# A recurrent layer and a gated wavelet layer: the first two steps' input product taken raw in fp32 column tiles

## The chip, the core and the metric

The kernel runs on one core of a Trainium2 chip. A core has five engines with instruction queues of their own: TensorE (PE in the profile, with its weight loads as PEld), VectorE (DVE), ScalarE (ACT), GpSimd (POOL) and SyncE (SP), which here only issues transfers. They meet at semaphores. Matmuls write into PSUM, eight banks of 128 partitions by 512 fp32 values; everything else lies in SBUF, 128 partitions wide, or in device memory, reached by 16 DMA engines.

The metric is the time of one execution on the device, in microseconds. Smaller is better.

## What is computed

There are 64 sequences of 256 steps with 1024 features each. The first layer is a recurrence with a residual, the second a Haar decomposition whose parts are all scaled by one gate and put together again, with a residual too:

```python
# layer 0
xW = jnp.einsum('ntd,dh->nth', x, Wx) + b
xW_t = jnp.swapaxes(xW, 0, 1)
def step(prev_h, xw):
    next_h = jnp.tanh(prev_h @ Wh + xw)
    return (next_h, next_h)
_, h_t = jax.lax.scan(step, h0, xW_t)        # h0 = cond_1024
x = x + jnp.swapaxes(h_t, 0, 1)
# layer 1
h = jax.nn.silu(q_pool @ W1.T + b1)          # q_pool = cond_1024
gate = jax.nn.sigmoid(h @ W2.T + b2)[:, None, :]
...
a = a * gate
for dc in reversed(details):
    dc = dc * gate
    e = (a + dc) * INV_SQRT2
    o = (a - dc) * INV_SQRT2
...
return v + a
```

Since every part of the decomposition is scaled by the same gate, layer 1 is a multiplication of x by 1 + gate. The kernel computes it so (its `factor` is that gate plus 1, times the residual of layer 0). What remains in order is the recurrence: step t needs the h of step t-1.

## The kernel before

**Layout.** Features lie on the partitions. A "pair" is two steps of all 64 sequences: a tile of 128 partitions by 1024, `pairs[i]`. T is 256 steps, NP 128 pairs, B = 8 blocks of 128 features, G = 2 groups of 32 sequences, Q = 4 quarters of 256 output features.

**Two ways to multiply.** A *column-tile* product (`plain_product`) takes 32 columns of its input as the stationary operand, and puts quarter q of the output on partitions 32q to 32q+31, so four quarters can stand in the array beside each other. One call covers one block k of features with 8 matmuls of 256 columns in fp32; the profile records each fp32 matmul twice. A *split* product (class `XWork`) cuts x and Wx into a high part and a scaled low part, types them for the faster fp32r matmul, and adds three products: main = x0·wx0 + x1·wx1, mixed = x2·wx2. One block is six matmuls of 128x512 and covers both steps of the pair; a pair is 48 of them. `split_weight` makes the three forms of a block of Wx, overwriting the raw block: on DVE L116, L133 and L135, on ACT L132 and L134. The constructor of `XWork` does the same for x (L116, L273, L275, and L281 on ACT in `begin`).

**From the split product to a step.** `take_mixed` scales the mixed banks into `sum` on ACT (L289) and POOL adds the bias row b_row (L290); `finish` adds the main banks on DVE (L321), writes `sum` to device memory and reads it back by eight transfers in the layout of h (L325, L331). `put` copies the result of one step into the bank `acc` (L225).

**A step.** `h_product` multiplies h by Wh with seven Strassen products of 32 records each into the banks acc, m16 and m57 (L183): products 1, 2, 5, 6, 7, 4, 3 in this order. Product 1 goes to m16, is copied by ACT into y[0] (L236), and product 6 is then accumulated in m16. DVE adds the parts (L242, L245, L249); ACT takes tanh (L426); DVE transposes (L428) and forms the four sums for the next step (`strassen_sides`, L213 to L216); POOL adds h to x (L455). The weights' own sums are made once: t5 from `first` (L164), t6, b12 and t4 from `others` (L164, L175, L164).

**The order.** PE's order is that of the program text throughout, DVE's until `in_order` is closed after step 0; a scheduler orders the rest. Between two step products PE works on the next pair: `first` (24 split matmuls) after an odd step, `second` (24) after an even one, so that a step's chain on DVE and ACT has something beside it. Step 0 has no Strassen product: `h_block` multiplies h0 by Wh in column tiles between the split blocks of pair 0. `gate_block` loads one block of W1 and multiplies h0 by it into `gate_ps`; `gate_hidden` applies b1 and silu, one block of W2 follows in each of steps 1 to 8, and `gate_factor` ends the gate.

**Buffers and queues.** A pool hands a tag's buffers out again when their last reader is done: tag `t` has six (raw Wx 0 to 5, then t5, t6, t4), `slab` six (x pairs, raw Wx 6 and 7, W1 and W2 blocks), `y` one (b1's tile first, then each step's y), `xw` three. Nearly all transfers are issued by SP in one order, with at most eight under way, since each takes the semaphore of the eighth before it; h0T, b_row and the tiles of b1 and b2 (eight small transfers each) are issued by ACT.

Of the kernel before, what the change touches and what calls it, by code (L numbers as in the profile page):

```python
# [59 lines left out]
P = 128  # L60
# [19 lines left out]
def tile_cond_resid(  # L80
# [26 lines left out]
    def slab(name: str):  # L107
        return slabs.tile([P, D], F32, tag="slab", name=name)

    def load_x(i: int) -> None:  # L110
        pairs[i] = slab(f"x{i}")
        nc.sync.dma_start(out=pairs[i], in_=xT[i])
# [9 lines left out]
    def load_weight(k: int):  # L122

        raw = sums_tile(f"wx{k}") if k < 3 * KB // 2 else slab(f"wx{k}")
        nc.sync.dma_start(out=raw, in_=wx[k])
        return raw

    def split_weight(raw, k: int) -> list:

        w0 = high_bits(raw[:], f"wx_high{k}")  # L130
        three = [wpool.tile([P, D], F32R, tag=f"wx{i}", name=f"wx{i}_{k}") for i in range(3)]
        nc.scalar.copy(three[0], w0)  # L132
        nc.vector.tensor_sub(raw, raw, w0)  # L133
        nc.scalar.activation(three[1], raw, AF.Copy, scale=UP)  # L134
        nc.vector.scalar_tensor_tensor(out=three[2], in0=raw, scalar=-UP, in1=w0, op0=ALU.mult, op1=ALU.add)  # L135
        return three

    def load_bias(v: bass.AP, pool, tag: str, name: str):
        t = pool.tile([P, G, F], F32, tag=tag, bufs=1, name=name)
        for q in range(Q):  # L140
            for g in range(G):
                nc.scalar.dma_start(out=t[q * R : (q + 1) * R, g, :], in_=v[q : q + 1, :].broadcast_to((R, F)))
        return t[:].rearrange("p g f -> p (g f)")

    def halves(w):
# [44 lines left out]
                    tile_position=(0, q * R),  # L190
                )

    def plain_product(ps, vT, w, k: int) -> None:

        for g in range(G):
            col = (g * B + k) * R
            for q in range(Q):


                nc.tensor.matmul(  # L200
                    out=ps[q * R : (q + 1) * R, g * F : (g + 1) * F],
                    lhsT=vT[:, col : col + R],
                    rhs=w[:, q * F : (q + 1) * F],
                    start=k == 0 and g == 0,
                    stop=k == B - 1,
                    skip_group_check=True,
                    tile_position=(0, q * R),
                )
# [10 lines left out]
    def flat(v):  # L219
        return v[:].rearrange("p i e -> p (i e)")  # L220
# [7 lines left out]
    def h_product(acc, a: dict, t: int):  # L228

        m16, m57 = (bank(f"m{i}", f"m{i}_{t}") for i in (16, 57))  # L230
        m16, m5, m7 = m16[:, :E], m57[:, :E], m57[:, E : 2 * E]
        part = [acc[:, i * E : (i + 1) * E] for i in range(3)]
        y = sums.tile([P, 4, E], F32, tag="y", bufs=1, name=f"y{t}")
        u = sums.tile([P, E], F32, tag="u", name=f"u{t}")
        strassen_product(m16, a[1], 1, True)
        nc.scalar.copy(y[:, 0], m16)  # L236
        strassen_product(part[0], a[2], 2)
        strassen_product(m5, a[5], 5, True)
        strassen_product(m16, a[6], 6)
        nc.scalar.copy(u, m16)  # L240
        strassen_product(m7, a[7], 7)
        nc.vector.tensor_add(  # L242
            y[:, 1:3], m57[:, : 2 * E].rearrange("p (i e) -> p i e", i=2), u[:].unsqueeze(1).broadcast_to((P, 2, E))
        )
        nc.vector.tensor_add(y[:, 3], m7, y[:, 1])  # L245
        strassen_product(part[2], a[4], 4)
        strassen_product(part[1], a[3], 3)
        h = work.tile([P, W], F32, tag="h", bufs=1, name=f"h{t}")
        nc.vector.tensor_add(h, acc, flat(y))  # L249
        return h  # L250

    def bank(tag: str, name: str):
        return one_pool.tile([P, HALF], F32, tag=tag, name=name)
# [81 lines left out]
            return xw  # L335


    h0T = const.tile([P, W], F32, tag="h0T", name="h0T")
    nc.scalar.dma_start(out=h0T, in_=condT)
    wh_raw = []  # L340
    b_row = const.tile([P, D], F32, tag="b_row", name="b_row")
    load_x(0)
    wx_raw, wx_s = [load_weight(k) for k in range(B)], []
    for k in range(B):
        wh_raw.append(wpool.tile([P, D], F32, tag="wh", name=f"wh_{k}"))
        nc.sync.dma_start(out=wh_raw[k], in_=wh[k])
    load_x(1)
    load_x(2)
    nc.scalar.dma_start(out=b_row, in_=b.broadcast_to((P, D)))
    b1_n = load_bias(b1, sums, "y", "b1_n")  # L350

    ctx.enter_context(tc.manual_schedule(engines={mybir.EngineType.PE}))
    in_order = ExitStack()
    in_order.enter_context(tc.manual_schedule(engines={mybir.EngineType.DVE}))
    now = XWork(0)
    now.begin()
    gate_ps = bank("gate", "gate_ps1")
    acc = bank("acc", "acc0")


    def h_block(k: int) -> None:
        plain_product(acc, h0T, wh_raw[k], k)

    def gate_block(k: int) -> None:
        w1 = slab(f"w1_{k}")
        nc.sync.dma_start(out=w1, in_=w1T[k])
        plain_product(gate_ps, h0T, w1, k)

    for k in range(B):
        wx_s.append(split_weight(wx_raw[k], k))  # L370
        now.block(k)
        if 3 <= k < 7:
            h_block(2 * k - 6)
            h_block(2 * k - 5)
    now.take_mixed()
    wh_s = StrassenWeight(wh_raw)
    wh_s.first()
    xw_next = now.finish()
    later = XWork(1)
    for k in range(B):  # L380
        gate_block(k)

    def gate_hidden(z):
        nc.vector.tensor_add(z, gate_ps, z)
# [26 lines left out]
        nc.gpsimd.tensor_mul(of_step(x, s), of_step(x, s), blocks(factor))  # L411

    h = work.tile([P, W], F32, tag="h", bufs=1, name="h0")
    nc.vector.tensor_add(h, acc, flat(xw_next[0]))
    now = later
    now.first()


    kept, again, factor = [], [], None
    for t in range(T):  # L420
        i, s = divmod(t, S)
        if s == 0:
            xw = xw_next
        if t:
            h = h_product(acc, sides, t)
        nc.scalar.activation(h, h, AF.Tanh)  # L426
        hT = work.tile([P, W], F32, tag="hT", name=f"hT{t}")
        nc.vector.transpose(hT, h)  # L428
        if t + 1 < T:
            sides = strassen_sides(hT, t)  # L430
        if t == 0:
            wh_s.others()
            g1T = gate_hidden(b1_n)
        if s == 0:
            acc = put(xw[1], t + 1)


        if s == 0 and i + 1 < NP:
            now.second()
            if i + 2 < NP:  # L440
                later = XWork(i + 2)
            xw_next = now.finish()
        if s == 1 and i + 2 < NP:
            now = later
            now.first()
        if s == 1 and i + 1 < NP:
            acc = put(xw_next[0], t + 1)

        if t == 0:
            in_order.close()  # L450


        x = pairs[i]
        if t + S < T:
            nc.gpsimd.tensor_add(of_step(x, s), of_step(x, s), blocks(hT))  # L455
        if 1 <= t <= B:
            k = t - 1
            if k == 0:
                gate_ps = bank("gate", "gate_ps2")
            w2 = slab(f"w2_{k}")  # L460
            nc.sync.dma_start(out=w2, in_=w2T[k])
            plain_product(gate_ps, g1T, w2, k)
            if k == B - 1:
                factor = gate_factor(load_bias(b2, const, "h0T", "b2_n"))
        if t + S >= T:

            for half in range(2):
                part = slice(half * KB, (half + 1) * KB)
                v = of_step(x, s)[:, :, part]
                nc.vector.tensor_add(v, v, blocks(hT)[:, :, part])  # L470
                nc.vector.tensor_mul(v, v, blocks(factor)[:, :, part])
                to = yT[i].rearrange("p (b s n) -> p s b n", b=B, s=S)[:, s, part]
                (nc.sync, nc.scalar)[half].dma_start(
                    out=to, in_=x[:].rearrange("p (b s n) -> p s b n", b=B, s=S)[:, s, part]
                )
        elif factor is not None:
            scale(x, s)
            if s == S - 1:
                nc.sync.dma_start(out=yT[i], in_=x)
        elif s == S - 1:  # L480
            kept.append(dram.tile([P, D], F32, tag="kept", bufs=B // S, name=f"kept{i}"))
            nc.sync.dma_start(out=kept[i], in_=x)
        if s == S - 1:
            del pairs[i]
            if i + 3 < NP:
                load_x(i + 3)


        if factor is not None and kept and i >= B and i % 4 < 2:
            if i % 4 == 0 and s == 0:  # L490
                again = slab(f"again{i}")
                nc.sync.dma_start(out=again, in_=kept[0])
            elif i % 4 == 1:
                scale(again, s)
                if s == 1:
                    nc.sync.dma_start(out=yT[i // 4 - B // 4], in_=again)
                    kept.pop(0)
# [28 lines left out]
```

## Time and profile before

| what | value |
| --- | --- |
| median of 3 runs | 3132.99 us (3133.29, 3128.22, 3132.99) |
| profiled execution | 3130.2 us, of which the span of its instructions is 3128.4 us |
| PE busy | 3080.6 us, 63648 matmul records |
| DVE, ACT, POOL busy | 1764.4, 718.7, 1113.9 us |
| DMA, mean over the span | 96 GB/s, 299.59 MB |
| first split matmul of pair 0 | 14.26 us |
| addition that starts h0 (DVE L414) | 52.08 us |
| first matmul of step 1's product | 70.14 us |
| first matmul of step 2's product, in the chain | 83.13 us |

A row of a timeline gives start, length, engine, line, operation, tiles written and read, and in brackets the engine's idle time before it with what ended it. A row of the chain that ended last gives start, length, and the engine or transfer on which the end rested. A row of a table of windows gives the window, its length, the busy time of the engine, the granted TensorE clock (1.00 is full speed), the share of the DMA engines and GB/s. PE's busy time overlaps itself, since matmuls are pipelined: for PE's pace the chain's lengths are used, not the single durations.

### The profile page before, as it was taken

Reading aid. Unit: us, or ns where it says so; the run is one execution under the profiler, and the core shown is the slowest. Engines: PE = TensorE matmul, PEld = TensorE weight load, DVE = VectorE, ACT = ScalarE, POOL = GpSimd, SP = SyncE. Lnnn points to the kernel's source line nnn. Section 1 sums busy time; section 2 is a strip of 40 time slices with the busy share of each in tenths; the row PEclk is TensorE's granted clock in tenths of the full one; section 3 lists DMA queues with packets and bytes.
Section 4 is the critical chain, followed back from the end, with each engine's and each line's share of the span. In section 5 each row is a group of like instructions: output and inputs, shape, how many; then the busy total and the mean of one; then the engine's idle time right before and its main releaser. Section 6 shows DMA issues by size and latency. Waiting matters only on the chain.

```text
span 3128.4 us, 137344 instructions
## 1 busy us (share of the span) xinstructions
PE 3080.6 (98%) x63648; PEld 2691.4 (86%) x63648; DVE 1764.4 (56%) x2736; ACT 718.7 (23%) x1425; POOL 1113.9 (36%) x768
## 2 busy tenths in 40 slices
PE   6999999999999999999999999999999999999998
PEld 4888888888888888888888888888888888888887
DVE  7455565555555555555555555555555555555554
ACT  3222222222222222222222222222222222222221
POOL 1233443333333333333333333333333333333332
PEclk9999999999999999999999999999999999999999
DMA  6332323222222222222222222222222222222222
GB/s 242 121 110 90 108 99 101 92 90 90 91 89 97 84 94 92 90 90 90 92 88 91 96 90 89 91 90 90 91 89 97 86 90 94 90 90 90 90 77 70
DMA packets 146573, 299.59 MB, mean 96 GB/s; under 512 B 25552, under 2 KB 91600, under 8 KB 146000
## 3 DMA queue, kind: packets, MB, share of 16 engines
q1 hardware_dynamic: 143888, 289.24, 27.3%
q8 instruction: 498, 8.16, 1.1%
q10 hardware_dynamic: 2112, 1.57, 0.2%
q14 instruction: 75, 0.61, 0.1%
HBM read 154.40 MB, written 136.31 MB: 93 GB/s over the span
## 4 chain that ended last, share of the span: by engine, by line
PE 95%; DMA 2%; DVE 1%; issue 1%; ACT 0%; SPq 0%; POOL 0%; ACTq 0%; DVEq 0%
PE main L257 29%; PE m L183 29%; PE acc L183 21%; PE mixed L257 15%; DMA sum_d<-sum 1%; DMA xw<-sum_d 1%; PE gate_ps L200 0%; DMA wx<-wx 0%; DMA w<-w1T 0%; PE acc L200 0%; DMA b_row<-b 0%; SPq L331 0%; DVE h L249 0%; DVE s L213 0%; ACT h L426 0%
## 5 line engine op out<-in xcount | busy, mean ns | idle before, releaser
L455 POOL TENSOR_TENSOR x<-x,hT 128x512 f32<-128x512 f32 x254 | 448.3, 1765 | 1691.2 <-DVE hT L428 1668.9
L257 PE MATMUL main<-wx,x 128*128 128x512 f32 x4096 | 990.5, 393 | 15.6 <-ACT wx L132 15.6
L257 PEld LDWEIGHTS main<-wx,x 128*128 128x128 f32 x4096 | 759.1, 188 | 196.5 <-issue 25.4
L242 DVE TENSOR_TENSOR y<-m,u 128x256 f32<-128x256 f32 x255 | 108.2, 425 | 872.4 <-PE m L183 872.4
L257 PE MATMUL mixed<-wx,x 128*128 128x512 f32 x2048 | 503.9, 398 | 2.1 <-DVE wx L135 2.1
L183 PE MATMUL m<-t,s 128*32 128x128 f32 x16320 | 493.4, 273 | 2.7 <-DVE s L215 2.7
L257 PEld LDWEIGHTS mixed<-wx,x 128*128 128x128 f32 x2048 | 374.4, 188 | 103.0 <-issue 25.8
L183 PEld LDWEIGHTS m<-t,s 128*32 128x32 f32 x16320 | 451.2, 110 | 3.5 <-issue 3.4
L290 POOL TENSOR_TENSOR sum<-sum,b_row 128x512 f32<-128x512 f32 x256 | 330.8, 1293 | 261.8 <-ACT sum L289 261.8
L426 ACT ACTIVATE h<-h 128x512 f32<-128x512 f32 x256 | 162.0, 633 | 800.3 <-DVE h L249 793.4
L411 POOL TENSOR_TENSOR x<-x,factor 128x512 f32<-128x512 f32 x246 | 334.4, 1359 | 15.4 <-DVE factor L397 5.7
L249 DVE TENSOR_TENSOR h<-acc,y 128x512 f32<-128x512 f32 x255 | 176.4, 692 | 242.4 <-PE acc L183 242.4
L428 DVE STREAM_TRANSPOSE hT<-h 128x512 f32<-128x512 f32 x256 | 182.3, 712 | 204.6 <-ACT h L426 204.6
L183 PEld LDWEIGHTS m<-wh,hT 128*32 128x32 f32 x8160 | 208.2, 109 | 92.7 <-issue 84.6
L275 DVE SCALAR_TENSOR_TENSOR x<-x,x_high 128x1024 fp32r<-128x1024 f32 x128 | 285.1, 2227 | 0.1
L183 PE MATMUL m<-wh,hT 128*32 128x128 f32 x8160 | 275.8, 276 | 4.6 <-DVE hT L428 4.6
L183 PE MATMUL acc<-wh,s 128*32 128x128 f32 x8160 | 272.6, 273 | 3.8 <-issue 3.7
L183 PE MATMUL acc<-wh,hT 128*32 128x128 f32 x8160 | 270.5, 273 | 4.7 <-ACT acc L225 4.7
L183 PE MATMUL acc<-t,hT 128*32 128x128 f32 x8160 | 269.9, 273 | 0.1
L183 PE MATMUL m<-wh,s 128*32 128x128 f32 x8160 | 269.6, 273 | 0.0
L281 ACT CAST x<-x_high 128x1024 fp32r<-128x1024 f32 x128 | 134.0, 1047 | 473.3 <-PE main L257 469.4
L183 PEld LDWEIGHTS acc<-wh,s 128*32 128x32 f32 x8160 | 229.3, 110 | 5.7 <-issue 5.7
(47 smaller groups left out, 2289.7 us busy)
## 6 DMA issues: line engine op xcount, KB each, us to landing
x<-xT SPq DMA_DIRECT2D x128, 512.0 KB, 3.7
sum_d<-sum SPq DMA_DIRECT2D x128, 512.0 KB, 3.1
xw<-sum_d SPq DMA_DIRECT2D x1024, 64.0 KB, 2.0
yT<-x SPq DMA_DIRECT2D x123, 512.0 KB, 3.6
wx<-wx SPq DMA_DIRECT2D x8, 512.0 KB, 6.9
wh<-wh SPq DMA_DIRECT2D x8, 512.0 KB, 10.2
w<-w1T SPq DMA_DIRECT2D x8, 512.0 KB, 4.2
w<-w2T SPq DMA_DIRECT2D x8, 512.0 KB, 3.9
```

Source lines behind the costliest of these rows:

```text
L183: nc.tensor.matmul(out=out[q * R : (q + 1) * R], lhsT=a[:, k * R : (k + 1) * R], rhs=wh_s.sides[i][k][:, q], start=first and k == 0, stop= ...
L242: nc.vector.tensor_add(y[:, 1:3], m57[:, : 2 * E].rearrange("p (i e) -> p i e", i=2), u[:].unsqueeze(1).broadcast_to((P, 2, E)))
L249: nc.vector.tensor_add(h, acc, flat(y))
L257: nc.tensor.matmul(out=acc[h], lhsT=v[:, k * P : (k + 1) * P], rhs=wx_s[k][which][:, h * HALF : (h + 1) * HALF], start=start and k == 0, s ...
L275: nc.vector.scalar_tensor_tensor(out=self.x2, in0=self.x1[:].bitcast(F32), scalar=-UP, in1=self.high, op0=ALU.mult, op1=ALU.add)
L281: nc.scalar.copy(self.x0, self.high)
L290: nc.gpsimd.tensor_add(s, s, b_row[:, h * HALF : (h + 1) * HALF])
L411: nc.gpsimd.tensor_mul(of_step(x, s), of_step(x, s), blocks(factor))
L426: nc.scalar.activation(h, h, AF.Tanh)
L428: nc.vector.transpose(hT, h)
L455: nc.gpsimd.tensor_add(of_step(x, s), of_step(x, s), blocks(hT))
```

## The change

Pair 0, steps 0 and 1, is no longer split. While raw Wx arrives, `x_block(k)` multiplies raw x of pair 0 by the raw block k in fp32 column tiles: step 0 into the bank acc, step 1 into the bank m57 under the name acc1_raw. The product of h0 and Wh is accumulated on top of step 0's in acc. The bias is a tile b_n in the layout of h, added by DVE to both banks. The split forms of Wx are first used by pair 1, whose 48 matmuls are put before step 1, two blocks of them between the raw blocks and six after step 0's h. The loads are reordered: x1 second, b and b_row behind Wh, W1 blocks 0 to 3 in the buffers of raw Wx 0 to 3, block 4 in a slab, blocks 5 to 7 after the last split. Small bias loads go through SP. At step 0 the acc of step 1 is now made by DVE from m57, and `others`, XWork(2) and `gate_hidden` follow in DVE's hand-written order.

```diff
     def load_bias(v: bass.AP, pool, tag: str, name: str):
-        t = pool.tile([P, G, F], F32, tag=tag, bufs=1, name=name)
+        t = pool.tile([P, G, F], F32, tag=tag, name=name)
         for q in range(Q):
             for g in range(G):
-                nc.scalar.dma_start(out=t[q * R : (q + 1) * R, g, :], in_=v[q : q + 1, :].broadcast_to((R, F)))
+                nc.sync.dma_start(out=t[q * R : (q + 1) * R, g, :], in_=v[q : q + 1, :].broadcast_to((R, F)))
...
-    def plain_product(ps, vT, w, k: int) -> None:
+    def plain_product(ps, vT, w, k: int, of=None, start: bool = True, stop: bool = True) -> None:
 
         for g in range(G):
-            col = (g * B + k) * R
+            col = of(g) if of else (g * B + k) * R
...
-                    start=k == 0 and g == 0,
-                    stop=k == B - 1,
+                    start=start and k == 0 and g == 0,
+                    stop=stop and k == B - 1,
...
-    wh_raw = []
     b_row = const.tile([P, D], F32, tag="b_row", name="b_row")
     load_x(0)
-    wx_raw, wx_s = [load_weight(k) for k in range(B)], []
+    load_x(1)
+    wx_raw, wx_s, wh_raw = [load_weight(k) for k in range(B)], [], []
     for k in range(B):
         wh_raw.append(wpool.tile([P, D], F32, tag="wh", name=f"wh_{k}"))
         nc.sync.dma_start(out=wh_raw[k], in_=wh[k])
-    load_x(1)
+    b_n = load_bias(b.rearrange("o (q f) -> (o q) f", q=Q), xwpool, "xw", "b_n")
+    nc.sync.dma_start(out=b_row, in_=b.broadcast_to((P, D)))
     load_x(2)
-    nc.scalar.dma_start(out=b_row, in_=b.broadcast_to((P, D)))
-    b1_n = load_bias(b1, sums, "y", "b1_n")
...
-    now = XWork(0)
+    now = XWork(1)
     now.begin()
-    gate_ps = bank("gate", "gate_ps1")
-    acc = bank("acc", "acc0")
-
+    acc, acc1, gate_ps = bank("acc", "acc0"), bank("m57", "acc1_raw"), bank("gate", "gate_ps1")
+
+    def x_block(k: int) -> None:
+        for s, ps in enumerate((acc, acc1)):
+            plain_product(ps, pairs[0], wx_raw[k], k, lambda g: (k * S + s) * N + g * R, stop=s == 1)
 
     def h_block(k: int) -> None:
-        plain_product(acc, h0T, wh_raw[k], k)
-
-    def gate_block(k: int) -> None:
-        w1 = slab(f"w1_{k}")
-        nc.sync.dma_start(out=w1, in_=w1T[k])
-        plain_product(gate_ps, h0T, w1, k)
+        plain_product(acc, h0T, wh_raw[k], k, start=False)
+
+    w1 = []
+
+    def load_w1(k: int) -> None:
+        w1.append(sums_tile(f"w1_{k}") if k < KB else slab(f"w1_{k}"))
+        nc.sync.dma_start(out=w1[k], in_=w1T[k])
+
+    def split_block(k: int) -> None:
+        wx_s.append(split_weight(wx_raw[k], k))
 
     for k in range(B):
-        wx_s.append(split_weight(wx_raw[k], k))
-        now.block(k)
-        if 3 <= k < 7:
-            h_block(2 * k - 6)
-            h_block(2 * k - 5)
-    now.take_mixed()
-    wh_s = StrassenWeight(wh_raw)
-    wh_s.first()
-    xw_next = now.finish()
-    later = XWork(1)
+        x_block(k)
+        split_block(k) if k < B - 1 else None
+        if k in (3, 5):
+            now.block(k // 4)
+    for k in range(KB + 1):
+        load_w1(k)
     for k in range(B):
-        gate_block(k)
+        h_block(k)
+    b1_n = load_bias(b1, sums, "y", "b1_n")
...
-    nc.vector.tensor_add(h, acc, flat(xw_next[0]))
-    now = later
-    now.first()
+    nc.vector.tensor_add(h, acc, b_n)
...
         if t == 0:
+            acc = bank("acc", "acc1")
+            nc.vector.tensor_add(acc, acc1, b_n)
+            split_block(B - 1)
+            for k in range(KB + 1, B):
+                load_w1(k)
+            for k in range(2, B):
+                now.block(k)
+            now.take_mixed()
+            wh_s = StrassenWeight(wh_raw)
+            wh_s.first()
+            xw_next = now.finish()
+            for k in range(B):
+                plain_product(gate_ps, h0T, w1[k], k)
             wh_s.others()
+            later = XWork(2)
             g1T = gate_hidden(b1_n)
-        if s == 0:
+            in_order.close()
...
+        elif s == 0:
             acc = put(xw[1], t + 1)
-
-
-        if s == 0 and i + 1 < NP:
-            now.second()
-            if i + 2 < NP:
-                later = XWork(i + 2)
-            xw_next = now.finish()
+            if i + 1 < NP:
+                now.second()
+                if i + 2 < NP:
+                    later = XWork(i + 2)
+                xw_next = now.finish()
```

In the diff, `k // 4` is 0 at k = 3 and 1 at k = 5, so the two early split blocks of pair 1 are blocks 0 and 1.

More of the change, by code (lines that the diff above doesn't have):

```diff
@@ L232, in h_product @@
         part = [acc[:, i * E : (i + 1) * E] for i in range(3)]
-        y = sums.tile([P, 4, E], F32, tag="y", bufs=1, name=f"y{t}")
+        y = sums.tile([P, 4, E], F32, tag="y", name=f"y{t}")
         u = sums.tile([P, E], F32, tag="u", name=f"u{t}")
@@ L421, in tile_cond_resid @@
         i, s = divmod(t, S)
-        if s == 0:
+        if s == 0 and t:
             xw = xw_next
@@ L431, in tile_cond_resid @@
         if t == 0:
+            acc = bank("acc", "acc1")
[11 more added lines that the diff above has]
+                plain_product(gate_ps, h0T, w1[k], k)
             wh_s.others()
+            later = XWork(2)
             g1T = gate_hidden(b1_n)
-        if s == 0:
+            in_order.close()
+        elif s == 0:
             acc = put(xw[1], t + 1)
-        if s == 0 and i + 1 < NP:
-            now.second()
-            if i + 2 < NP:
-                later = XWork(i + 2)
-            xw_next = now.finish()
+            if i + 1 < NP:
[3 more added lines that the diff above has]
+                xw_next = now.finish()
         if s == 1 and i + 2 < NP:
@@ L447, in tile_cond_resid @@
             acc = put(xw_next[0], t + 1)
-        if t == 0:
-            in_order.close()
         x = pairs[i]
```

## Prediction

> **What bounds the kernel now.** I read the page's shares first, then the chain that ended last, then the first 84 us of that chain in order of time, since everything the change touches lies there.
>
> ```profile
> PE 3080.6 (98%) x63648; PEld 2691.4 (86%) x63648; DVE 1764.4 (56%) x2736; ACT 718.7 (23%) x1425; POOL 1113.9 (36%) x768
> ...
> PE 95%; DMA 2%; DVE 1%; issue 1%; ACT 0%; SPq 0%; POOL 0%; ACTq 0%; DVEq 0%
> ```
>
> The tensor engine (PE) carries 95% of the chain. The other 5% is nearly all start-up. In the chain (start, length, what):
>
> ```profile
> 30.26 1.86 PE acc L200 x32
> ...
> 51.67 3.74 DMA w<-w1T
> 55.41 0.04 issue
> 55.45 3.64 PE gate_ps L200 x32
> 59.09 3.87 PE mixed L257 x16
> 62.96 7.25 PE main L257 x32
> 70.22 1.01 PE m L183 x32
> ...
> 76.47 3.85 PE mixed L257 x16
> 80.32 1.81 PE main L257 x8
> 82.13 1.00 PE gate_ps L200 x16
> 83.13 0.87 PE m L183 x32
> ```
>
> The reader should see three things. Until 55 us PE waits for weights and W1; step 1's product starts at 70.22; step 2's starts at 83.13 and from there PE is solid. In the two programs the order of each engine's instructions is the same from step 2 on, apart from the eight small loads of b2, which go to SP's queue. So **the change is worth 83.13 minus the time at which the changed kernel starts step 2's product.**
>
> **The change, part by part.**
>
> *PE work.* Removed: pair 0's 48 split matmuls, 8 blocks of 6 at 0.227 us (7.25/32), 10.9 us. Added: 8 raw blocks of 16 column-tile matmuls, each recorded twice. The nearest row is the 1.86 us for 32 records above (same tile, 256 columns, fp32), so 1.86 a block and 14.9 in all. PE's work grows by 4.0 us; a gain can come only from idle time.
>
> *Loads.* x1 now goes ahead of Wx, while b and its row copies leave the ACT queue and follow Wh. Before wx0 lie h0T (0.26 MB), x0, x1 and wx0 itself (0.52 each): 1.83 MB. The queues moved 154 GB/s in the first 4 us and 400 in the next 4, so wx0 is here at 0.62 MB by 4.0, plus 1.21/0.4 = 3.0, plus 0.5 to land: 7.5 us. Each later 512 KB takes 1.28 us (SP's issues stand 1.28 apart from 18.13 on): wx7 at 16.5, wh7 at 26.7, then b, b_row, x2 and w1_0 to w1_4 by about 38. All of it is ahead of its use below.
>
> *Raw x and h0.* PE runs from 7.5: the first block at the half clock, 3.8 us; seven at 1.86, 13.0; two split blocks between them at 1.6 (0.66+0.47+0.46 in the chain), 3.2; eight h blocks at 0.93, 7.4. End: 34.9. Beside it VectorE (DVE) splits Wx; each split now overwrites raw Wx, so it waits for its raw block. Only the first does (until 11.3); then 1.23+1.23 for the rest of it and six more at 3.30 give 33.7. PE is last, by 1.2 us. The round trip of pair 0 through DRAM (sum out, eight xw loads; 44.3 to 52.1) is gone: h0 starts at 35.0 against 52.08.
>
> *The chain on DVE after h0.* This part is late next. The rows:
>
> ```profile
> 56.34 2.49 DVE L164 TENSOR_TENSOR t<-wh,t 128x512 f32<-128x512 f32 x4
> ...
> 61.85 2.95 POOL L290 TENSOR_TENSOR sum<-sum,b_row 128x512 f32<-128x512 f32 x1 [6.23 <-ACT sum L289]
> ...
> 63.57 0.68 DVE L384 TENSOR_TENSOR b_n<-gate_ps,b_n 128x512 f32<-128x512 f32 x1
> 64.32 1.28 ACT L386 ACT_TABLE_LOAD   x1 [2.54 <-DVE b_n L384]
> ...
> 66.28 0.69 DVE L387 TENSOR_TENSOR s<-s,b_n 128x512 f32<-128x512 f32 x1 [2.03 <-ACT s L386]
> ```
>
> DVE's order in the changed kernel is fixed by hand: h0, transpose, sides (4.35 from the add to the last side, 52.08 to 56.42, with ACT's tanh and POOL's first x addition inside it), 39.35; the new addition for step 1's acc, 0.7, 40.05; the split of wx7, 3.2, 43.3; t5, 2.45, 45.75. Then the two L321 additions, which need POOL's. POOL can start at 44.5 (block 7's mixed matmuls, 0.42, and ACT's 0.7 after 43.3), beside t5. The row at 61.85 shows what that costs: 2.95 us beside such DVE additions, ending 1.2 after them, against 1.30 when alone. So POOL ends at 47.0, its second at 48.3, and the L321s at 49.1 instead of 47.9. Then t6, b12 and t4, 7.3 (56.34 to 63.65): 56.4; the split of x2, 3.2: 59.6; gate_hidden to its product, 3.4 (63.57 to 66.97, a table load inside): **63.0**.
>
> *The wait that this makes.* b1's tile and step 1's y share one single buffer (tag y). The copy m16 to y[0] (L236) therefore waits until gate_hidden's product has read b1, and product 6, which overwrites m16, waits for that copy. Before, gate_hidden was over at 66.97 and L236 ran at 71.35; the wait cost nothing. Now PE reaches product 6 sooner: blocks 2 to 7 end at 43.9; gates 0 to 4 at 48.6; w1_5 and w1_6 land by 46.7 (w1_6 goes out when wx7 is split, plus 3.6); w1_7's slab comes free with gate 4, so it lands at 52.2 and the gate ends at 53.2. Products 1, 2 and 5 take 2.7: 55.8. **PE then stands from 55.8 to 63.4.** Queued behind it are products 6, 7, 4, 3 and all of pair 2's first half; h1, and so step 2, waits for them.
>
> *The clock after that hole.* [...] The row (window, PE busy, granted clock as the third-last figure):
>
> ```profile
> 46.00:48.00 2.00, 0.39 (x8) 1.00 0.79 205
> 48.00:50.00 2.00, 0.33 (x4) 0.70 1.00 407
> 50.00:52.00 2.00, 2.00 (x24) 0.50 0.81 221
> ...
> 56.00:58.00 2.00, 2.00 (x24) 0.50 0.64 244
> 58.00:60.00 2.00, 2.00 (x16) 0.74 0.66 201
> ```
>
> After 3.28 us idle (46.4 to 49.67) PE ran at half clock, and work unbroken from 55.45 stayed there to about 59.0. [...] by the row 3.6/2 = 1.8; by the kernel's first matmuls (14.26 to 19.0) 2.4. I take 2.0. So the four products, 3.5 warm, end at 63.4+5.5 = 68.9, and step 2 follows after the same 6.7 as before (76.4 to 83.13): **75.6**. h1 is transposed by 71.2 and stays hidden under pair 2's first half.
>
> *At nothing.* The mode changes between full and column tiles are fewer (about 0.2 us each in the chain, 0.66 against 0.47). b1 and b2 on SP are covered by PE-bound steps; if not, each issue is 0.4 us of queue.
>
> **Sum:** 83.13 - 75.6 = 7.5 us. The profiled execution took 3130.2 (span 3128.4), so 3122.7. That execution is 2.8 under the median of the runs shown (3132.99), which spread over 5.1; from the median it would be 3125.5. I keep 3122.7.
>
> **Rivals.**
> 1. *No hole: step 1 runs through.* If the y copy doesn't hold PE, step 1 runs from 53.2 to 59.3; the next limit is h1's chain behind gate_hidden on DVE (transposed near 67.5), so step 2 starts at 67.5: 15.6 gained, 3114.6. For it: in the trace L236 follows its product at once. Against it: the one buffer, and ACT's sigmoid ahead of L236 in order. 0.12.
> 2. *The DVE chain is longer.* It holds some thirty instructions between 35 and 63, and each lost us goes straight to the end. DVE L214 took 1.35 us beside POOL's addition against 0.29 alone; three more such meetings, a raw phase 1.5 us later and a longer cold stretch make 4 to 7 us: 3127 to 3130, within the noise. 0.20.
> 3. *Slower: raw blocks don't pack.* If the 16 matmuls of a raw block, which alternate between two banks, ran two abreast rather than four, a block is 3.7 us and h0 comes 14.9 later: 3122.7+14.9 = 3137.6. It decides from 2.8 us a block (break-even). Against it: the h blocks pack in the same form at 1.86 per 32 records. 0.05.
>
> The likeliest case keeps 0.63. Its bounds: restart 0 to 3.5 us (no loss, or all four products at half clock), POOL's overlap 0 to 1.2, raw phase 1 either way: 3118 to 3127.
>
> **Chances.** A measurement of this kernel can't tell less than about 0.2% (6.3 us) from no change. The likeliest case lies beyond 0.2% in most of its range (0.55 of its 0.63), rival 1 wholly (0.12), rival 2 a little (0.02): faster 0.69. Same: 0.08+0.17+0.01 = 0.26. Slower 0.05. The range 3114 to 3130 takes in rival 1 and most of rival 2.
>
> **What would show it.** Right: wx raw blocks at 1.86 us; h0's addition near 35; PE idle before m16's product 6 in step 1, released by ACT's y copy at about 63; granted clock 0.5 after it; step 2's product at about 75.6. Wrong: L200's matmuls on wx at 3 us a block; or no idle before product 6; or a new stall after step 2, where I count none.

## The result, and the profile after

| | before | after |
| --- | --- | --- |
| median | 3131.85 us (3128.22 to 3133.29, 4 runs) | 3114.18 us (3112.97 to 3118.69, 4 runs) |
| profiled execution, span | 3130.2, 3128.4 us | 3118.69, 3116.8 us |
| first matmul of step 2's product | 83.13 us | 75.78 us |

The change makes the kernel faster by half a per cent: the ratio of the times is 0.9948, with a 95% interval of 0.9931 to 0.9965, that is 16.3 us of 3131.85 (11 to 22). The two profiled executions lie 11.5 us apart. Of the four runs of the changed kernel the profiled one is the longest, 4.5 us over the median.

The page of the changed kernel: the shares by engine, those of the chain that ended last, the queue that brings instructions, and the one group of matmuls that now has a long wait in front of it (busy us, mean ns; idle us before it and what ended most of it).

```profile
PE 3080.9 (99%) x63856; PEld 2696.6 (87%) x63856; DVE 1762.4 (57%) x2732; ACT 715.4 (23%) x1421; POOL 1109.1 (36%) x766
...
q8 instruction: 500, 8.19, 1.1%
...
PE 95%; DMA 2%; DVE 1%; issue 0%; ACT 0%; SPq 0%; POOL 0%; DVEq 0%; ACTq 0%; POOLq 0%
...
L183 PE MATMUL m<-t,s 128*32 128x128 f32 x16320 | 497.4, 274 | 8.2 <-ACT y L236 5.7
```

At this height almost nothing moves. The last row names one wait of 5.7 us for ACT's copy at L236, and it stands in step 1. The timeline there shows it:

```profile
7.85 1.94 PE L200 MATMUL acc<-wx,x 128*32 128x256 f32 x16 [7.85 <-DMA wx<-wx]
...
35.16 0.69 DVE L418 TENSOR_TENSOR h<-acc,b_n 128x512 f32<-128x512 f32 x1 [0.88 <-DMA x<-xT]
...
44.54 3.37 POOL L290 TENSOR_TENSOR sum<-sum,b_row 128x512 f32<-128x512 f32 x2 [5.79 <-ACT sum L289]
...
53.28 1.07 PE L200 MATMUL gate_ps<-w,h0T 128*32 128x256 f32 x16 [2.58 <-DMA w<-w1T]
...
61.61 0.69 DVE L391 TENSOR_TENSOR s<-s,b_n 128x512 f32<-128x512 f32 x1 [2.02 <-ACT s L390]
62.39 0.27 ACT L236 COPY y<-m 128x128 f32<-128x128 f32 x1 [0.81 <-DVE s L391]
62.71 1.93 PE L183 MATMUL m<-t,s 128*32 128x128 f32 x32 [5.74 <-ACT y L236]
```

These are the steps of the prediction in order: wx0's landing, h0's addition, POOL's two additions, w1_7's landing, and then the wait. DVE's product at L391 is the last reader of b1's tile; ACT's copy to y follows at once, and PE's product 6 at once after the copy. (The row of h0's addition names a load of x, which ended at 35.15; PE's h blocks ended at 35.10, and in a second execution the same row names PE.) The chain from there to step 2:

```profile
62.71 3.64 PE m L183 x64
66.35 2.77 PE acc L183 x64
69.11 3.85 PE mixed L257 x16
72.97 1.81 PE main L257 x8
74.78 1.00 PE gate_ps L200 x16
75.78 0.87 PE m L183 x32
```

The start is thus 7.35 us shorter. The spans differ by 11.6. So some 4.3 us come from a place where the prediction counted nothing: behind step 2's start. In the kernel before, steps 5 to 8 each hold a pause of PE inside a product, and the changed kernel has none there. From the timeline of PE before:

```profile
128.81 0.42 PE L183 MATMUL acc<-wh,s 128*32 128x128 f32 x5 [1.13 <-issue]
...
142.54 0.64 PE L183 MATMUL acc<-wh,s 128*32 128x128 f32 x14 [0.75 <-issue]
...
156.33 0.85 PE L183 MATMUL acc<-wh,s 128*32 128x128 f32 x22 [0.81 <-issue]
...
169.82 1.08 PE L183 MATMUL acc<-wh,s 128*32 128x128 f32 x31 [0.58 <-issue]
```

"issue" says that nothing which the profile shows held PE, and each row is the rest of a product cut in two: 5, 14, 22 and 31 of its 32 matmul records come behind the pause. The rest grows by about 9 from step to step. PE's own records (weight loads, matmuls and its semaphore instructions), numbered from 0 at the start, show a pattern: the pauses stand at numbers 3265, 3777, 4289 and 4801, which are all 193 above a multiple of 256 ("place 193" below). From the start of the last instruction before to the start of the first one after they are 1.40, 1.02, 1.08 and 0.85 us long, 4.35 together. In this kernel queue q8, which brings instructions, moved 8.16 MB in 498 pieces, 16.4 KB each, and PE has 127561 records, 256 for each piece. The pieces come to PE as it goes on: one started at 126.33 and took 0.88 us, and PE stood from 127.41 to 128.81. Before step 2 the changed kernel has 413 more of PE's records (1653 against 1240), which is 157 above a multiple of 256: behind them the borders of the pieces fall elsewhere in every product.

### The profile page after: what moved, and what is told of

It reads as the page before. It is cut to its first block, busy times and chain, and to the rows that moved or that the text cites. A ratio compares the mean times of both kernels' runs of the same rounds, so it can differ in the third digit from the quotient of the medians.

```text
span 3116.8 us, 137762 instructions
## 1 busy us (share of the span) xinstructions
PE 3080.9 (99%) x63856; PEld 2696.6 (87%) x63856; DVE 1762.4 (57%) x2732; ACT 715.4 (23%) x1421; POOL 1109.1 (36%) x766
## 4 chain that ended last, share of the span: by engine, by line
PE 95%; DMA 2%; DVE 1%; issue 0%; ACT 0%; SPq 0%; POOL 0%; DVEq 0%; ACTq 0%; POOLq 0%
PE main L257 29%; PE m L183 29%; PE acc L183 21%; PE mixed L257 15%; DMA sum_d<-sum 1%; DMA xw<-sum_d 0%; DMA wh<-wh 0%; DMA x<-xT 0%; DMA wx<-wx 0%; SPq L331 0%; PE gate_ps L200 0%; ACT h L428 0%; DVE hT L430 0%; DVE h L249 0%; DMA yT<-x 0%
## 5 line engine op out<-in xcount | busy, mean ns | idle before, releaser
L183 PEld LDWEIGHTS acc<-wh,hT 128*32 128x32 f32 x8160 | 228.6, 110 | 5.5 <-ACT acc L225 5.5
```

The lines of the kernel that those rows point to most:

```text
L183: nc.tensor.matmul(out=out[q * R : (q + 1) * R], lhsT=a[:, k * R : (k + 1) * R], rhs=wh_s.sides[i][k][:, q], start=first and k == 0, stop= ...
```

## The experiments

**Theory A:** the gain has two parts: the earlier start (7.4 us), and the pauses of steps 5 to 8, which went because the count of PE's instructions ahead of them changed. **Theory B:** the pauses are chance, or belong to something else in the start, and the whole gain is the earlier start. The first four kernels ran on one chip beside the kernel before (median 3130.27 us, 35 runs).

**Shift the count and nothing else.** Into the idle time of PE in the first microseconds of the kernel before go 39 small matmuls, whose result nobody reads; in the changed kernel 25 go in behind the seventh block of the gate. PE's records grow by 156 and by 100, which puts each kernel within one record of where the other one was.

```diff
+    def pad(n: int) -> None:
+        ps = bank("m16", "pad")
+        for j in range(n):
+            q = j % Q
+            nc.tensor.matmul(out=ps[q * R : (q + 1) * R, :R], lhsT=h0T[:, :R], rhs=h0T[:, :R],
+                start=True, stop=True, skip_group_check=True, tile_position=(0, q * R))
...
+    pad(39)
     for k in range(B):
         wx_s.append(split_weight(wx_raw[k], k))
```

```diff
             for k in range(B):
                 plain_product(gate_ps, h0T, w1[k], k)
+                if k == 6:
+                    pad(25)
```

> The kernel before, unchanged, for the spread of its time and a second look at its trace. Fetch theory (PE's instructions come in 16 KB pieces of 256, and PE pauses where a new piece is needed in the middle of a dense Strassen product): the same four pauses in steps 5 to 8, at the same instructions (number 193 of a piece), 4 to 4.5 us together, and step 2's product at about 83.1 us. Chance theory (the pauses were an accident of transfers in that one execution): fewer, or elsewhere. Time within 0.1% of the runs of before.

> The kernel before with 39 small matmuls into an unused bank while PE waits for the first weights: they shift every later PE instruction by 156 places, which sets the pieces of 256 where the changed kernel has them. Fetch theory: step 2 stays at about 83.1 us, the four pauses in steps 5 to 8 go, and the time falls by 4.3 us (0.14%). Rival (the pauses come from transfers that collide with the b2, W2 and x loads of these steps): the pauses stay, no change.

> The changed kernel, unchanged, for the spread of its time and a second look at its trace. Step 2's product at about 75.8 us again, PE idle for about 5.7 us ahead of product 6 of step 1, no pause in steps 5 to 8. If the 5 us by which its profiled execution was longer than the others was an accident of stalls in steps 13 to 38, these are fewer now. Time 3113 to 3116 us.

> The changed kernel with 25 small matmuls into an unused bank, put where PE waits for the last block of W1: they shift every later PE instruction by 100 places, which sets the pieces of 256 where the kernel before has them. Fetch theory: step 2 stays at about 75.8 us, four pauses of 0.8 to 1.4 us appear in steps 5 to 8, and the time rises by 3 to 4.5 us over the changed kernel. Rival (the pauses are tied to transfers, b2's queue among them, which the change moved): no pauses, no change.

| kernel | median us | ratio to before, 95% | step 2 starts | pauses at place 193 over 0.5 us, steps 5 to 9 |
| --- | --- | --- | --- | --- |
| before, again | 3131.02 (13 runs) | 1.0004 (0.9996 to 1.0013) | 84.25 | 0.54, 1.02, 1.86, 1.45, 0.60 |
| before, shifted | 3125.01 (21 runs) | 0.9986 (0.9979 to 0.9992) | 83.78 | none |
| after, again | 3114.45 (5 runs) | 0.9952 (0.994 to 0.9964) | 75.66 | none (one of 0.78 in step 2) |
| after, shifted | 3119.47 (7 runs) | 0.997 (0.9959 to 0.998) | 73.56 | 1.27, 1.10, 0.90, 0.96 |

The waits of PE from step 2 to the end (us in total, times, longest), first of the kernel before, then of the same kernel shifted:

```profile
PE acc L183 <- ACT acc L225: 4.7, 5, 2.4
PE m L183 <- DVE hT L428: 4.6, 2, 2.3
PE acc L183 <- issue: 3.7, 5, 1.1
PE m L183 <- DVE s L215: 2.7, 3, 1.2
```

```profile
PE m L183 <- DVE hT L444: 4.6, 2, 2.3
PE acc L183 <- ACT acc L225: 3.5, 3, 2.0
PE m L183 <- DVE s L215: 2.7, 3, 1.2
```

The row "issue" is gone, the others stay within 1.2 us. The shift leaves the start where it was (83.78 lies between 83.13 and 84.25) and takes 4.4 us off the time (2.5 to 6.6 by the interval). The opposite shift brings the pauses into the changed kernel. In its timeline of PE three of them cut the same products of steps 5 to 7 almost where they were cut before; the fourth comes in step 9, in product 4:

```profile
119.12 0.42 PE L183 MATMUL acc<-wh,s 128*32 128x128 f32 x6 [1.00 <-issue]
...
132.91 0.64 PE L183 MATMUL acc<-wh,s 128*32 128x128 f32 x14 [0.83 <-issue]
...
146.40 0.86 PE L183 MATMUL acc<-wh,s 128*32 128x128 f32 x23 [0.63 <-issue]
...
172.83 0.43 PE L183 MATMUL acc<-t,hT 128*32 128x128 f32 x8 [0.69 <-issue]
```

This kernel starts step 2 2.1 us sooner than the changed one, which was not expected; 1.3 us of that stand already at h0's addition (33.83 instead of 35.16), long before the small matmuls run. It is 5.0 us slower all the same, and each of its runs is slower than each of the five unshifted ones. Its four pauses are 4.2 us of that; the rest is open. Theory B falls, and with it the rival that loads collide in these steps, since the shifts left the loads as they were: a few dozen matmuls that compute nothing move the time by 4 to 5 us in either direction.

The traces also tell when a pause comes. There are as many pieces as places 193 (498 of each in the kernel before), so they can be paired in order. In all eleven traces, from 70 us to the end, PE never gets past a place sooner than 1.2 us after the transfer of its piece has ended. The 13 pauses of the table and of the kernel before end 1.2 to 1.6 us after that transfer, short ones and long ones alike; PE had come to the place between 0.5 us before the transfer's end and 0.9 us after it. In the shifted kernel before and in the changed one, which have no such pause, PE came to the places of steps 5 to 9 1.5 us or more after the transfer. So these pauses are PE waiting for its next instructions. This is read from the traces; no run moved the transfers alone.

The two kernels run again show how far one execution repeats. The four pauses of the kernel before came back at the same numbers, 4.9 us together, with a fifth in step 9. In the changed kernel the wait ahead of product 6 was 3.89 us, not 5.74: the clock had already fallen to half in products 1 and 2 (0.52 at 56 to 58 us), so PE came later to the same hole, whose end (62.60) and step 2's start (75.66) stayed.

**The wait for b1's tile.** The prediction's hole in step 1 has one cause: y and b1 share a buffer. Two kernels take it away in different manners. The first gives b1 a buffer of its own, the second leaves the buffer shared and lets `gate_hidden` go ahead of the split of x2 in DVE's order. A third asks about another part of the change, the early loads of W1: it loads every block of W1 just ahead of its use, into slabs, as before. They ran beside the kernel before at 3129.91 us (9 runs).

```diff
-    b1_n = load_bias(b1, sums, "y", "b1_n")
+    b1_n = load_bias(b1, sums, "b1y", "b1_n")
```

```diff
-            later = XWork(2)
             g1T = gate_hidden(b1_n)
+            later = XWork(2)
```

```diff
     def load_w1(k: int) -> None:
-        w1.append(sums_tile(f"w1_{k}") if k < KB else slab(f"w1_{k}"))
+        w1.append(slab(f"w1_{k}"))
...
-    for k in range(KB + 1):
-        load_w1(k)
...
-            for k in range(KB + 1, B):
-                load_w1(k)
...
             for k in range(B):
+                load_w1(k)
                 plain_product(gate_ps, h0T, w1[k], k)
```

> The changed kernel with a buffer of its own for b1's tile, so that step 1's y no longer waits for gate_hidden. Hole theory (PE waits 4 to 6 us ahead of product 6 of step 1 for ACT's copy of m16, which waits for b1's buffer, and restarts at half clock): no idle of PE ahead of product 6, granted clock at 1.0 there, and step 2's product at about 67.5 us (now bound by h1's chain on DVE, which stands behind gate_hidden) against 75.7: the time falls by about 8 us to 3106. Rival (the split of x2 or the gate's end holds step 2 anyway): step 2 at 73 to 76 us, a gain under 3 us.

> The changed kernel with gate_hidden ahead of the split of x2 in DVE's order, same buffers. Hole theory: the copy of m16 comes at 59.4 instead of 62.3 us, so PE idles about 2.7 us ahead of product 6[...]; its first half of pair 2 waits for the split of x2 at 63; step 2's product at about 69.9 us, the time falls by 5.8 us to 3108.7. If the clock had cost nothing, the gain would be 3 us. Rival (the hole is hidden by what follows): no change.

> The changed kernel with W1 loaded as before, one block behind the other through the slabs; its two last blocks are then issued behind the eight xw loads of pair 1. Hole theory: the gate ends near 62 to 63 us instead of 54, gate_hidden and the copy of m16 follow at 66 to 67, step 2's product at 77 to 79 us: slower by 1.5 to 3.5 us. Rival (W1's place is worth the whole gain of the change): step 2 near 83 us, slower by 7 us.

| kernel | median us (5 runs each) | ratio to before, 95% | step 2 starts |
| --- | --- | --- | --- |
| b1 in its own buffer | 3107.97 (3107.19 to 3108.93) | 0.9929 (0.9916 to 0.9943) | 67.93 |
| gate first | 3108.83 (3107.47 to 3110.97) | 0.9933 (0.992 to 0.9945) | 69.59 |
| W1 loaded late | 3118.82 (3117.46 to 3123.57) | 0.9967 (0.9954 to 0.9979) | 77.63 |

With its own buffer, b1 no longer holds PE: there is no idle time before product 6, and step 2 starts 7.9 us sooner than in the changed kernel. Of the kernels tried this one has the lowest median, below both given ones; against the changed kernel the two intervals just touch (0.9943 and 0.994), though no run of the one reaches a run of the other. The start times are near what was expected, but what then bounds the start is not DVE's chain to h1. The chain of the first kernel goes through the last block of W1:

```profile
48.20 4.17 DMA w<-w1T
52.37 0.04 issue
52.41 1.41 PE gate_ps L200 x16
53.82 1.71 PE m L183 x32
55.52 1.37 PE acc L183 x32
56.90 2.62 PE m L183 x96
59.52 1.75 PE acc L183 x64
61.26 3.85 PE mixed L257 x16
```

PE waits for w1_7 until 52.4, and product 1 then takes 1.71 us where a warm one (at full clock) takes 0.87: the windows of PE there read 0.50 (third-last figure).

```profile
50.00:52.00 2.00, 0.00 (x0) 1.00 0.95 283
52.00:54.00 2.00, 1.59 (x25) 0.75 1.02 412
54.00:56.00 2.00, 2.00 (x47) 0.50 0.98 367
```

With the gate first, ACT's copy comes at 58.91, and product 6 waits only a little:

```profile
59.23 1.08 PE L183 MATMUL m<-t,s 128*32 128x128 f32 x32 [1.06 <-ACT y L236]
```

The expectation had 2.7 us here and counted no loss at a restart; but 2.47 us of waiting for w1_7 had lowered the clock before (0.50 at 54 to 56 us), so PE came later. One move in DVE's hand-written order is worth as much as the buffer, within what can be measured. In the kernel with W1 loaded late the last blocks of W1 wait for slabs and then stand behind the reading back of xw in SP's queue, and the gate, and with it b1's tile, is late:

```profile
57.15 4.25 DMA w<-w1T
61.40 0.04 issue
61.44 1.98 PE gate_ps L200 x16
...
66.94 0.28 ACT y L236
67.22 0.04 issue
67.26 1.96 PE m L183 x64
```

So the early loads of W1 are worth about 2 us of start in the changed kernel (77.63 against 75.7), and the medians agree in sign (3118.82 against 3114.2 and 3114.5), though only part of that difference is the start.

**The last block of W1 sooner.** Since w1_7 is what PE waits for when b1 has its own buffer, the last two kernels bring it sooner, into a buffer that raw Wx leaves free, one with b1's buffer of its own and one with the buffer shared. They ran beside the kernel before at 3127.92 us (9 runs).

```diff
-        w1.append(sums_tile(f"w1_{k}") if k < KB else slab(f"w1_{k}"))
+        w1.append(sums_tile(f"w1_{k}") if k < KB or k == B - 1 else slab(f"w1_{k}"))
```

> own_y, with the last block of W1 in one of the buffers of raw Wx too, so that it no longer waits for a slab. In own_y the chain ran through that block's landing (52.4 us) and a cold restart. Now it lands near 48.5, PE has no wait there and stays at full clock, and step 2's product is bound by h1's chain behind gate_hidden on DVE: 66.4 us against 67.9. Time 1.5 us under own_y, 3106.5. Rival (own_y was bound by DVE already): step 2 at 67.9, no change.

> The changed kernel with the same edit alone. Hole theory: the end of the hole is set by gate_hidden on DVE, and the gate's end had 4 to 5 us to spare, so PE only waits longer ahead of product 6: step 2's product at 75.7 us, give or take 1 for the clock, and no change of time (0.1%). Rival (W1's last block carries the start): step 2 about 2 us sooner.

With the buffer shared, 3115.58 us (ratio 0.996, 0.9947 to 0.9972) and step 2 at 75.89: nothing gained, as expected, since PE only waits longer at the next place.

```profile
63.13 1.94 PE L183 MATMUL m<-t,s 128*32 128x128 f32 x32 [9.14 <-ACT y L236]
```

With b1's own buffer it was a miss: 3109.32 us (3105.82 to 3111.05; ratio 0.9935, 0.9921 to 0.9948), and step 2 at 68.61, later than without the edit and 2.2 us later than expected. The timeline shows where:

```profile
55.96 0.61 PE L183 MATMUL acc<-t,hT 128*32 128x128 f32 x14
58.67 0.71 PE L183 MATMUL acc<-t,hT 128*32 128x128 f32 x17 [2.09 <-issue]
```

PE stands for 2.4 us in the middle of product 4, from 56.3 to 58.67, at its record number 1473, which is again 193 above a multiple of 256; a piece of instructions started at 56.25, when PE had come to record 1470, and took 0.92. In the changed kernel and with b1's own buffer alone the piece at 56 us started at record 1271 and 1207, since PE had waited longer before. The clock then falls to 0.50 at 60 us. The kernel with b1's own buffer alone passes the same number in the same product without a pause: there the transfer ended at 56.62 and PE came to the number 3.0 us later; here it ended at 57.17, 0.9 us after PE had come, and PE went on 1.5 us after it. That the pause makes the miss is read from the trace, and wasn't tried by a shift.

## Why the prediction was right, and what it missed

| step | predicted | measured |
| --- | --- | --- |
| wx0 is here, raw phase begins | 7.5 | 7.85 |
| first raw block; each later one | 3.8; 1.86 | 3.4 by its matmul rows; 2.95 for the second, then 1.73 |
| h0's addition | 35.0 | 35.16 |
| split of wx7 ends | 43.3 | 43.3 |
| t5 ends | 45.75 | 46.8 |
| POOL's second addition ends | 48.3 | 47.9 |
| w1_7 is here | 52.2 | 53.3 |
| split of x2 ends | 59.6 | 59.0 |
| product L391 over, b1's tile free | 63.0 | 62.3 |
| PE stands ahead of product 6 | 7.6 | 5.74 |
| product 6 begins | 63.4 | 62.71 |
| loss at the cold restart | 2.0 | 2.9 |
| step 2's product | 75.6 | 75.78 |

In the first row, the 0.5 us "to land" was an estimate; in the profile of before the last signal of a transfer comes 0.40 us after the last packet (median of the 303 places where no packet follows for 1.5 us; 0.27 to 1.04). In the second row, the first block ran at half pace: its two rows of 16 records took 1.94 and 1.97 us, the rows from 14.18 us on 1.05.

**The earlier start was right by its own steps.** DVE's chain of some thirty instructions came out 0.7 us shorter than summed: t5 took 3.58 us instead of 2.45 beside POOL, but the L321 additions behind it then had little to wait for. The hole for b1's buffer is there, and the two kernels that take it away or shorten it show that it cost 6 to 8 us of start; so "the y copy doesn't hold PE" falls as a rival. Raw blocks took 1.73 us each, not the 3.7 of the slower case, so that falls too.

**The cold restart was mis-sized.** The four products took 69.11 - 62.71 = 6.4 us against 3.5 warm. That is 2.9 lost, above the 2.0 taken, an estimate between the 1.8 and 2.4 that the profile of before gave, and within the bound of 3.5. The windows of PE show half clock from 62 to 68 us:

```profile
60.00:62.00 2.00, 0.00 (x0) 0.87 0.89 267
62.00:64.00 2.00, 1.29 (x27) 0.50 0.09 31
64.00:66.00 2.00, 2.00 (x44) 0.50 0.00 0
66.00:68.00 2.00, 2.00 (x44) 0.50 0.03 8
68.00:70.00 2.00, 2.00 (x40) 0.92 0.00 0
```

So the start time was right to 0.2 us because two errors cancelled: 0.9 us more lost at the restart, 0.7 us less on DVE's chain.

**The step that failed** is the frame of the sum: "the change is worth 83.13 minus the time at which the changed kernel starts step 2's product", argued from the same order of each engine's instructions from step 2 on. "From there PE is solid" was not so: the four pauses were in the profile of before, as part of the 1% of "issue" in the chain, and the sum put them at nothing. The order behind step 2 is the same, but not the count of instructions ahead of it, and PE's instructions come in pieces of 256. The shift alone is worth 4.4 us in the kernel before. With it the sum is 7.35 + 4.4 = 11.8, and the profiled executions differ by 11.5, a closer match than single executions, which scatter by some us, can promise.

**The range held by luck.** The median of 3114.18 is 8.5 us under the forecast of 3122.7, below the 3118 to 3127 of the likeliest case, and 0.2 us inside the stated range. The range reached down to 3114 for the sake of rival 1, in which PE doesn't wait for b1's tile; that rival fell. What filled its place was the four pauses, and some us that stay open.

**Left open.** The medians differ by 16.3 us here and by 15.8 in the second measurement, with intervals that reach down to 11; the two parts cover 11.8. Most of the remaining 4 us goes with the granted clock, averaged over a run. In the second measurement the kernel before was at 0.998 in 4 of 35 runs (median 3126.5) and at 0.997 or less in the others; the changed kernel was at 0.998 in 4 of 5 (median 3114.1). At the same 0.998 they differ by 12.4 us. What lowers the clock no run takes apart, and the cold start is part of the average. One way stands in the profiled execution of the changed kernel: a stall of 2.34 us that ended at 422.47 was followed by half clock for 3.4 us (windows: 0.82, 0.50, 0.82), which is 1.7 us lost. That execution was 4.5 us over the median of its kernel. Stalls of PE for copies of acc and for DVE's sums come to 7.4 us in the profile of before and 6.6 in that of after, and to 8.0 and 6.3 in the second executions.

## What to carry to other kernels

When a change adds or takes away instructions ahead of a long stretch that is bound by one engine, look for short pauses put down to "issue" in that stretch, and number the engine's instructions: if the pauses stand at one place within the pieces in which they come (256 here), a few instructions in idle time can move them, and part of a measured gain or loss may be nothing else. When work is moved earlier, ask of each small shared buffer on its way who read it last before and who reads it last now: a wait that had cost nothing became 5.7 us of idle PE and a cold restart. One more buffer took it away, and one line moved left 1.1 us of it.

## What was not expected of the hardware

- PE stood for 0.5 to 2.4 us at place 193 of every 256 of its records in some of the column-tile products where that place fell. It went on 1.2 to 1.6 us after the transfer of a piece of instructions had ended, and 39 small matmuls in idle time changed a time of 3130 us by 4.4.
- The clock fell to half after idle times of 2.1 to 2.8 us: 2.54 us before the gate's last block with b1's own buffer, 2.47 with the gate first (windows at 54 to 56 us: 0.50), 2.75 at the same place in the second execution of the changed kernel (0.52 at 56 to 58), and 2.09 at the pause of the kernel with both edits (0.50 at 60 to 62). In the first execution of the changed kernel a wait of 2.58 us there left it at 1.00. The trace of the prediction had half clock after 3.28 us; here less was enough, and what decides, these runs don't show.
